# Macaron block on one core: joint quantised norms of two tiles, biases added by GpSimd, scales as two-tensor operations of VectorE

## The chip, the cores and the metric

The kernel runs on one core of a Trainium2 chip. The metric is the device time of one execution in microseconds (us). A time is given as the median of several runs, and one further execution was taken with the hardware profiler. "TensorE" is PE in the profile (its weight loads are PEld), "VectorE" is DVE, "ScalarE" is ACT, "GpSimd" is POOL, and SP is the engine that issues nearly all DMAs.

## The reference, cut to what matters

The input x is 4 x 4096 x 512 in float32, which is 128 tiles of 128 rows. Three sublayers follow each other, each on a layer norm of x:

```python
x = x + 0.5 * ffn(layernorm(x), weight, bias)
x = x + attention(layernorm(x), qkv_w, qkv_b, rpb, proj_w, proj_b)
x = x + 0.5 * ffn(layernorm(x), weight, bias)      # the same weights again

def ffn(x, weight, bias):
    xq, xs = mx_quantize(x)          # blocks of 32 columns: scale = max|block| / 7.5,
    wq, ws = mx_quantize(weight)     # values rounded to the nearest of the FP6 (E2M3) grid
    return (xq * xs) @ (wq * ws).T + bias
```

The attention has 16 heads of 32 columns. Each query sees the 13 keys around it, with a relative bias `rpb`, a softmax, and an output projection by `proj_w` with bias `proj_b`.

## The kernel before, in words

**Products.** Every large product is done in float16 with each operand split into a high and a low part. `product` (L147) issues 12 matmuls of 128x512 into one PSUM tile: low by high, high by low, high by high, four chunks of 128 columns each. Where it has a bias, a thirteenth matmul goes first (L151): a matrix of ones times a bfloat16 tile whose first three rows hold the bias split in three. The FFN (result tile pmf) and the output projection (pmo) have this, the values (pmv) and queries and keys (pmqk) do not. All these results share three PSUM tiles.

**Order of the work.** The order on every engine is written out by hand. The program is a list of slots; a stage is a generator that begins in a slot and says, with each `yield n, rank`, how many slots later it goes on and at which rank within that slot. `run_slot` (L170) runs what is due, lowest rank first, and the engines execute in that order. One step is `STEP = 7` slots, and one tile begins in each step. In the even stretch each step holds stages of several tiles: the first FFN of one tile, the values of an earlier one, an attention item (a group of 512 rows and 4 heads: scores ps at L408, a softmax, the product with the values pv at L478), the output projection of a tile some 13 steps older, and that tile's second FFN.

**The quantised norm.** Both FFNs use `quantised_norm` (L216), once for each tile and FFN. The first FFN's norm is called n1, the second's n3; the plain norm in front of the attention is n2. The stages of one quantised norm are these:

- VectorE: moments of x (L185, L187).
- GpSimd: three operations on one column, giving scale and shift (`factors`, L193, L196, L198).
- ScalarE: the normed tile y (L203).
- VectorE: the greatest magnitude of each block of 32 (L226), a `tensor_scalar` that makes the block's scale of it (L227), a reciprocal (L231).
- GpSimd: y times the reciprocal (L233).
- ScalarE: rounding by a cast to fp8 (L236).
- GpSimd: the fp8 values times the scale (L238).
- ScalarE: the high part (`high`, L208).
- VectorE: the low part (`low`, L213), after which SP issues a DMA that transposes both parts (L214). TensorE reads the transposed tile, xT.

n1 begins 11 slots before its tile's own slot and its product comes 8 slots after its transpose. n3 follows the projection: `project_out` (L516) evicts pmo into x (L525, VectorE) and goes on with the norm in the same stage. The second FFN begins `F2 = 12` slots after the projection, which leaves three slots between the transpose of n3 and the first weight load of its product. n1 and n3 of a step are separate chains of instructions, a slot apart or interleaved. Where this text says "the low part" it means L213, of n1, n2 or n3.

**The softmax.** For each item VectorE adds up the scores from PSUM with the table (L433, L436), takes the maximum of each block (L440), GpSimd subtracts it (L442), ScalarE takes the exponential (L444), VectorE sums (L447), takes the reciprocal (L448) and scales it by a constant with a `tensor_scalar` (L449), GpSimd multiplies (L451), ScalarE writes the high part twice (L455, L456) and GpSimd the low part (L458). SP then transposes the probabilities (pT, L460). The values come back from DRAM by the loads called vs (L384).

**Setup.** Before the slots begin, the FFN weights are quantised (L674 to L720), and `put_bias` (L579) splits the FFN bias in three bfloat16 rows (L583, L585) and sends each into `ffn_bias` by a DMA (L586); the same is done for the attention's bias at L767 to L770.

Of the kernel before, what the change touches and what calls it, by code (L numbers as in the profile page):

```python
# [37 lines left out]
P = 128  # L38
# [12 lines left out]
QB = 32  # L51
# [13 lines left out]
def macaron_kernel(  # L65
# [41 lines left out]

    nudge = const.tile([P, 1], F32, name="nudge")
    nc.gpsimd.memset(nudge, -(2.0 ** -28) * (1 + 2.0 ** -10))
    minus_half = const.tile([P, 1], F32, name="minus_half")  # L110
    nc.gpsimd.memset(minus_half, -0.5)


    wt = const.tile([P, 2, KC, 5 * dim], F16, name="wt")


    ones = const.tile([P, P], BF16, name="ones")
    nc.gpsimd.memset(ones, 1.0)
    ffn_bias = const.tile([P, dim], BF16, name="ffn_bias")
    att_bias = const.tile([P, dim], BF16, name="att_bias")  # L120
    nc.gpsimd.memset(ffn_bias, 0.0)
    nc.gpsimd.memset(att_bias, 0.0)
    qk_b = const.tile([P, 2, KC], F32, name="qk_b")
    coef = const.tile([P, 4], F32, name="coef")
    cf, cp, alpha = coef[:, 0:1], coef[:, 1:2], coef[:, 2:3]
# [4 lines left out]
    def bc(t, n):  # L130

        return t.unsqueeze(2).to_broadcast([t.shape[0], t.shape[1], n])

    def blocks(t):
        return t.rearrange("p (n q) -> p n q", q=QB)
# [8 lines left out]
        ti = t.bitcast(I32)  # L144
        nc.vector.tensor_scalar(ti, ti, 1, None, ALU.bitwise_or)

    def product(pm, lhs, rhs, bias=None):  # L147

        n = 0
        if bias is not None:  # L150
            nc.tensor.matmul(pm, ones, bias, start=True, stop=False)  # L151
            n = 1
        last = n + 3 * KC - 1
        for a, b in ((0, 1), (1, 0), (0, 0)):
            for c in range(KC):
                nc.tensor.matmul(  # L156
                    pm, lhs(a, c), rhs(b, c), start=(n == 0), stop=(n == last)
                )
                n += 1

# [6 lines left out]
    def begin(slot, stage, rank=5):  # L167
        slots.setdefault(slot, []).append((rank, stage))
# [11 lines left out]
        xs[t] = xp.tile([P, dim], F32, tag="x", name=f"x{t}")  # L180
        nc.sync.dma_start(out=xs[t], in_=xf[t * P : (t + 1) * P, :])

    def statistics(t, which):
        st = sm.tile([P, 6], F32, tag=f"st{which}", name=f"st{which}_{t}")
        nc.vector.bn_stats(st, xs[t])  # L185
        mv = sm.tile([P, 2], F32, tag=f"mv{which}", name=f"mv{which}_{t}")
        nc.vector.bn_aggr(mv, st)  # L187
        return mv

    def factors(t, which, mv):  # L190

        rs = sm.tile([P, 1], F32, tag=f"rs{which}", name=f"rs{which}_{t}")
        nc.gpsimd.tensor_scalar(  # L193
            rs, mv[:, 1:2], XS ** -2, LN_EPS * XS ** -2, ALU.mult, ALU.add
        )
        nc.gpsimd.tensor_tensor(rs, rs, minus_half, ALU.pow)  # L196
        nb = sm.tile([P, 1], F32, tag=f"nb{which}", name=f"nb{which}_{t}")
        nc.gpsimd.tensor_scalar(nb, mv[:, 0:1], rs, -1.0, ALU.mult, ALU.mult)  # L198
        return rs, nb

    def normed(t, which, rs, nb):
        y = yp.tile([P, dim], F32, tag=f"y{which}", bufs=1 if which == "n2" else 2, name=f"y{which}_{t}")
        nc.scalar.activation(y, xs[t], AF.Identity, bias=nb, scale=rs)  # L203
        return y

    def high(y, which, t):
        hl = hlp.tile([P, 2, dim], F16, tag=f"hl{which}", name=f"hl{which}_{t}")
        nc.scalar.copy(hl[:, 0, :], y)  # L208
        return hl

    def low(y, hl, dst):

        nc.vector.tensor_tensor(hl[:, 1, :], y, hl[:, 0, :], ALU.subtract)  # L213
        nc.sync.dma_start_transpose(out=dst, in_=hl.rearrange("p s k -> p (s k)"))  # L214

    def quantised_norm(t, which, wait=1):  # L216

        mv = statistics(t, which)
        yield wait, 1
        rs, nb = factors(t, which, mv)  # L220
        yield 1, 1
        y = normed(t, which, rs, nb)
        yield 1, 1
        yb = blocks(y)
        sc = sm.tile([P, NB], F32, tag=f"sc{which}", name=f"sc{which}_{t}")
        nc.vector.tensor_reduce(sc, yb, AX.X, ALU.max, apply_absolute_value=True)  # L226
        nc.vector.tensor_scalar(  # L227
            sc, sc, F8_SCALE / Q_MAX, F8_SCALE * XS * Q_EPS, ALU.mult, ALU.max
        )
        r = sm.tile([P, NB], F32, tag=f"r{which}", name=f"r{which}_{t}")  # L230
        nc.vector.reciprocal(r, sc)  # L231
        yield 1, 1
        nc.gpsimd.tensor_tensor(yb, yb, bc(r, QB), ALU.mult)  # L233
        yield 1, 1
        q8 = q8p.tile([P, dim], F8, tag=f"q8{which}", name=f"q8_{which}_{t}")
        nc.scalar.activation(q8, y, AF.Identity, bias=nudge, saturate=False)  # L236
        yield 1, 3
        nc.gpsimd.tensor_tensor(yb, blocks(q8), bc(sc, QB), ALU.mult)  # L238
        yield 1, 3
        hl = high(y, which, t)  # L240
        yield 1, 1
        xT = xtp.tile([P, 2, KC, P], F16, tag=f"xT{which}", name=f"xT{which}_{t}")
        low(y, hl, xT.rearrange("p s c q -> p (s c) q"))
        ys[t] = xT

    def ffn(t, which):

        xT = ys.pop(t)
        pm = ps_m.tile([P, dim], F32, tag="mm", name=f"pm{which}_{t}")
        product(  # L250
            pm, lambda s, c: xT[:, s, c, :], lambda s, c: wt[:, s, c, FO : FO + dim], ffn_bias
        )
        yield 1, 8
        nc.vector.scalar_tensor_tensor(xs[t], pm, cf, xs[t], ALU.mult, ALU.add)  # L254

    def first_half(t):

        yield from ffn(t, "f1")
        mv = statistics(t, "n2")
        yield 2, 2  # L260
        rs, nb = factors(t, "n2", mv)
        yield 1, 2
        y = normed(t, "n2", rs, nb)
        hl = high(y, "n2", t)
        yield 1, 2
        g, i = divmod(t, GROUP)
        if i == 0:
            x2[g] = x2p.tile([P, 2, KC, GROUP, P], F16, tag="x2", name=f"x2_{g}")
        low(y, hl, x2[g][:, :, :, i, :].rearrange("p s c q -> p (s c) q"))
# [122 lines left out]
    def softmax(m):  # L392
# [53 lines left out]
        total = sm.tile([P, MAXB], F32, tag="total", name=f"total{m}")  # L446
        nc.vector.tensor_reduce(total[:, :n], s, AX.X, ALU.add)  # L447
        nc.vector.reciprocal(total[:, :n], total[:, :n])  # L448
        nc.vector.tensor_scalar(total[:, :n], total[:, :n], PS, None, ALU.mult)  # L449
        yield 1, 4  # L450
        nc.gpsimd.tensor_tensor(s, s, bc(total[:, :n], KN), ALU.mult)  # L451
        yield 2, 8
# [60 lines left out]
                ALU.mult, ALU.subtract,  # L513
            )

    def project_out(t):  # L516

        r = t * P % RING
        pm = ps_m.tile([P, dim], F32, tag="mm", name=f"pmo_{t}")
        product(  # L520
            pm, lambda s, c: ring[:, s, c, r : r + P], lambda s, c: wt[:, s, c, PO : PO + dim],
            att_bias,
        )
        yield 1, 8
        nc.vector.scalar_tensor_tensor(xs[t], pm, cp, xs[t], ALU.mult, ALU.add)  # L525
        yield from quantised_norm(t, "n3")

    def second_half(t):

# [5 lines left out]

    F1, V, QK, SC, PV, OUT, F2 = 6, 2 * STEP + 1, 5 * STEP + 3, 6 * STEP, 8 * STEP + 3, 13 * STEP + 2, 12

    def one(f, *args):
        f(*args)
        return  # L540
        yield

    free = (n_items - 1) * STEP + PV + 3
    for t in range(NT):
        k = t * STEP
        begin(k - 18, one(load, t), 0)
        begin(k - 11, quantised_norm(t, "n1", 2), 1)
        begin(k + F1, first_half(t))
        begin(k + V, values(t))

        at = k + OUT
        if at > free:
            at = free + 4 * ((at - free) // STEP)
        begin(at, project_out(t))
        begin(at + F2, second_half(t))
    for m in range(n_items):
        k = m * STEP
        begin(k + QK, project_qk(m))
        begin(k + SC, softmax(m), 6)
        begin(k + PV, attend(m), 6)  # L560
# [7 lines left out]
    with tc.tile_pool(name="setup", bufs=1) as sp, tc.tile_pool(name="scratch", bufs=2) as scr:  # L568
# [2 lines left out]
        rp = sp.tile([HEADS, NREL + 2 * (QR - 1)], F32, name="rp")  # L571
        for o in range(KC):
            nc.sync.dma_start(out=fw[:, o, :], in_=ffn_w[o * P : (o + 1) * P, :])
        fb = sp.tile([1, dim], F32, name="fb")
        pb_ = sp.tile([1, dim], F32, name="pb_")
        nc.scalar.dma_start(out=fb, in_=ffn_b.unsqueeze(0))
        nc.scalar.dma_start(out=pb_, in_=proj_b.unsqueeze(0))

        def put_bias(out, b, name):  # L579

            for i in range(3):
                part = sp.tile([1, dim], BF16, name=f"{name}{i}")
                nc.vector.tensor_copy(part, b)  # L583
                if i < 2:
                    nc.vector.tensor_tensor(b, b, part, ALU.subtract)  # L585
                nc.sync.dma_start(out=out[i : i + 1, :], in_=part)  # L586

        nc.scalar.dma_start(out=b12, in_=qkv_b.rearrange("(c p) -> c p", p=P))
        nc.gpsimd.memset(rp, 0.0)
        nc.scalar.dma_start(out=rp[:, QR - 1 : QR - 1 + NREL], in_=rpb)  # L590
# [56 lines left out]

        powers(4, 5)
        nc.vector.tensor_scalar(cf, down[:, 4:5], 0.5 / XS, None, ALU.mult)
        nc.vector.tensor_scalar(fb, fb, up[:1, 4:5], XS, ALU.mult, ALU.mult)  # L650
        put_bias(ffn_bias, fb, "fb")

        def put_weights(o, hl):
            return nc.sync.dma_start_transpose(
# [103 lines left out]
        def attention_bias():  # L758
# [5 lines left out]
            pmb = ps_m.tile([P, dim], F32, tag="mm", name="pmb")  # L764
            product(pmb, lambda s, c: vbx[:, s, c, :], lambda s, c: wt[:, s, c, PO : PO + dim])
            yield 1, 9
            for e in (su[:1, 2:3], su[:1, 3:4], XS):  # L767
                nc.vector.tensor_scalar(pb_, pb_, e, None, ALU.mult)
            nc.vector.tensor_tensor(pb_, pmb[:1, :], pb_, ALU.add)
            put_bias(att_bias, pb_, "ab")  # L770

# [93 lines left out]
```

## Time and profile before

| what | value |
|---|---|
| median of three runs | 2516.75 us (2513.81 to 2518.8) |
| the profiled execution | 2513.41 us, of which 2511.3 us is the span from first to last instruction |
| granted TensorE clock, mean of the span | 0.986 |
| TensorE, busy | 2382.7 us (95%) |
| VectorE, busy | 2148.2 us (86%) |
| GpSimd, busy | 1601.0 us (64%) |
| ScalarE, busy | 1370.1 us (55%) |
| DMA queue q1, share of 16 engines | 78.0% |

The shares are averages over the whole span. The first 250 us or so (setup, and the first tiles, whose attention has not begun) and the last 170 us (no new tiles) run differently from the long even stretch between them, in which one step of seven slots follows the other. Numbers of a group (line, engine, operation, tiles) give the count, the total busy time and the mean duration of one instruction; the latter includes any time in which the instruction had begun and stood still.

### The profile page before, as it was taken

The numbers are of one execution on the slowest core, as the hardware profiler recorded it, in microseconds if no ns is written. First come the engines' busy times: TensorE is split into PE (matmuls) and PEld (weight loads), VectorE is DVE, ScalarE is ACT, GpSimd is POOL, SyncE is SP. The second block draws the span as 40 slices with busy tenths as digits, with TensorE's granted clock in tenths as the row PEclk, the third lists the DMA queues.
The fourth block names the chain that finished last, engine by engine and source line by source line (L and its number), as shares of the span: only waits on it lengthen the run. The fifth ranks groups of instructions, "written<-read, shape, count | busy, mean of one in ns | idle before, by whom it ended". The sixth has DMA issues, their size and how long they took to land.

```text
span 2511.3 us, 84309 instructions
## 1 busy us (share of the span) xinstructions
PE 2382.7 (95%) x35923; PEld 1158.1 (46%) x35923; DVE 2148.2 (86%) x4052; ACT 1370.1 (55%) x2306; POOL 1601.0 (64%) x2082
## 2 busy tenths in 40 slices
PE   1799999999999999999999999999999999999877
PEld 0244444444444444444444444444444444444432
DVE  8688998989988898898988889888998989888654
ACT  4455555555555555555555555555555555555432
POOL 4456666666666666666666666666666666666443
PEclk9899999999999999999999999999999999999988
DMA  6589888788878878887887887787888789877752
GB/s 162 123 138 142 151 152 153 144 148 153 152 138 151 152 143 148 155 146 141 154 155 138 147 156 144 149 152 149 143 149 155 142 149 154 153 141 139 120 85 70
DMA packets 929237, 360.22 MB, mean 143 GB/s; under 512 B 722654, under 2 KB 893530, under 8 KB 928860
## 3 DMA queue, kind: packets, MB, share of 16 engines
q1 hardware_dynamic: 928800, 354.81, 78.0%
q8 instruction: 281, 4.60, 0.8%
q14 instruction: 96, 0.79, 0.1%
q10 hardware_dynamic: 60, 0.01, 0.0%
HBM read 109.62 MB, written 67.29 MB: 70 GB/s over the span
## 4 chain that ended last, share of the span: by engine, by line
PE 80%; DVE 10%; DMA 6%; ACT 2%; issue 1%; POOL 1%; SPq 0%; ACTq 0%; DVEq 0%; POOLq 0%
PE pmf L156 22%; PE pmqk L156 22%; PE pmv L156 13%; PE pmo L156 12%; PE ps L408 6%; DMA xTn<-hln 5%; PE pv L478 3%; PE pmf L151 2%; DMA x<-hln 2%; DVE stn L185 1%; DVE scn L227 1%; PE pmo L151 1%; DVE scn L226 1%; DVE x L254 1%; ACT qk L344 1%
## 5 line engine op out<-in xcount | busy, mean ns | idle before, releaser
L156 PE MATMUL pmf<-wt,xTn 128*128 128x512 f16 x3072 | 723.0, 386 | 56.9 <-DMA xTn<-hln 56.8
L156 PE MATMUL pmqk<-x,wt 128*128 128x512 f16 x3072 | 705.9, 380 | 0.0
L156 PEld LDWEIGHTS <-xTn 128*128 128x128 f16 x3072 | 302.7, 99 | 437.7 <-DMA xTn<-hln 70.0
L156 PEld LDWEIGHTS <-wt 128*128 128x128 f16 x3072 | 290.6, 98 | 337.1 <-issue 1.5
L156 PE MATMUL pmv<-wt,x 128*128 128x512 f16 x1536 | 365.0, 389 | 23.6 <-DMA x<-hln 23.0
L458 POOL TENSOR_TENSOR p<-sf,p 128x714 f16<-128x714 f32 (+2 forms) x128 | 192.1, 1501 | 265.5 <-ACT p L455 265.5
L233 POOL TENSOR_TENSOR yn<-yn,rn 128x512 f32<-128x512 f32 x256 | 270.0, 1055 | 132.3 <-DVE rn L231 127.8
L156 PE MATMUL pmo<-wt,ring 128*128 128x512 f16 x1536 | 352.7, 379 | 0.6 <-issue 0.4
L236 ACT ACTIVATE q_n<-yn,nudge 128x512 fp8e4<-128x512 f32 x256 | 184.8, 722 | 292.5 <-POOL yn L233 292.5
L505 ACT ACTIVATE ring<-pv 128x510 f16<-128x510 f32 (+8 forms) x224 | 82.4, 414 | 470.5 <-PE pv L478 468.9
L203 ACT ACTIVATE yn<-x,nbn,rsn 128x512 f32<-128x512 f32 x384 | 313.8, 817 | 37.5 <-POOL nbn L198 37.5
L193 POOL TENSOR_SCALAR rsn<-mvn 128x1 f32<-128x1 f32 x384 | 122.5, 319 | 309.7 <-DVE mvn L187 299.1
L196 POOL TENSOR_TENSOR rsn<-rsn,minus_half 128x1 f32<-128x1 f32 x384 | 252.4, 657 | 32.0
L185 DVE BATCH_NORM_STATS2 stn<-x 128x6 f32<-128x512 f32 x384 | 265.2, 691 | 8.8
L348 DVE SCALAR_TENSOR_TENSOR qk<-pmqk,qk_b,qk 128x512 f16<-128x512 f32 x256 | 191.2, 747 | 89.9 <-ACT qk L344 89.9
L238 POOL TENSOR_TENSOR yn<-q_n,scn 128x512 f32<-128x512 fp8e4 x256 | 263.1, 1046 | 3.3 <-ACT q_n L236 3.3
L213 DVE TENSOR_TENSOR hln<-yn,hln 128x512 f16<-128x512 f32 x384 | 250.5, 678 | 5.4 <-ACT hln L208 4.9
L227 DVE TENSOR_SCALAR scn<-scn 128x16 f32<-128x16 f32 x256 | 241.3, 943 | 8.8
L451 POOL TENSOR_TENSOR sf<-sf,total 128x714 f32<-128x714 f32 (+2 forms) x128 | 178.6, 1395 | 96.8 <-DVE total L449 90.0
L156 PEld LDWEIGHTS <-ring 128*128 128x128 f16 x1536 | 150.1, 98 | 182.7 <-issue 2.4
L208 ACT CAST hln<-yn 128x512 f16<-128x512 f32 x384 | 225.3, 616 | 9.5 <-POOL yn L238 3.2
L156 PEld LDWEIGHTS <-x 128*128 128x128 f16 x1536 | 142.5, 99 | 189.2 <-DMA x<-hln 25.7
(114 smaller groups left out, 3042.0 us busy)
## 6 DMA issues: line engine op xcount, KB each, us to landing
vs<-vd SPq DMA_DIRECT2D x144, 357.0 KB
x<-in_L_attn_x_dram SPq DMA_DIRECT2D x128, 256.0 KB
vd<-vt SPq DMA_DIRECT2D x128, 256.0 KB
out_dram<-x SPq DMA_DIRECT2D x128, 256.0 KB
vs<-vd SPq DMA_DIRECT2D x24, 378.0 KB
vs<-vd SPq DMA_DIRECT2D x24, 315.0 KB
xTn<-hln SPq DMA_TRANSPOSE x256
rows<-in_L_attn_qkv_w_dram SPq DMA_DIRECT2D x12, 256.0 KB
```

What stands on the lines that cost most here:

```text
L156: nc.tensor.matmul(pm, lhs(a, c), rhs(b, c), start=(n == 0), stop=(n == last))
L185: nc.vector.bn_stats(st, xs[t])
L196: nc.gpsimd.tensor_tensor(rs, rs, minus_half, ALU.pow)
L203: nc.scalar.activation(y, xs[t], AF.Identity, bias=nb, scale=rs)
L208: nc.scalar.copy(hl[:, 0, :], y)
L213: nc.vector.tensor_tensor(hl[:, 1, :], y, hl[:, 0, :], ALU.subtract)
L227: nc.vector.tensor_scalar(sc, sc, F8_SCALE / Q_MAX, F8_SCALE * XS * Q_EPS, ALU.mult, ALU.max)
L233: nc.gpsimd.tensor_tensor(yb, yb, bc(r, QB), ALU.mult)
L236: nc.scalar.activation(q8, y, AF.Identity, bias=nudge, saturate=False)
L238: nc.gpsimd.tensor_tensor(yb, blocks(q8), bc(sc, QB), ALU.mult)
L348: nc.vector.scalar_tensor_tensor(t[:, s, 1, KN:], pms[s], bias, t[:, s, 0, KN:], ALU.add, ALU.subtract)
L458: nc.gpsimd.tensor_tensor(p[:, :n, KN : 2 * KN], s, ph, ALU.subtract)
```

## The change

Three things are changed together.

- **Joint norms.** n1 of one tile and n3 of another, where both fall into the same slot, become one piece of work (`quantised_norms`). The moments of each tile are still taken separately (`moments`), into one tile of two columns. From there on each stage handles both: the factors on two columns (four GpSimd operations instead of two times three), two ScalarE activations into one y of 128x1024, and then single operations on 1024 columns or 32 block scales, and one DMA that transposes 16 blocks. At the start of the program, where there is no n3 yet, and at its end, where there is no n1, a joint tile holds one tile.
- **Biases.** The bias matmuls go, and the setup that split the biases. The half FFN bias and the attention's bias are kept in float32 in all partitions, and GpSimd adds them to x (`add_bias`): three operations of 128x512 a tile, one ahead of each addition of a sublayer's result.
- **Scales.** The two `tensor_scalar` operations of VectorE (L227 and L449) become a `scalar_tensor_tensor` with the constant tile `least` and a `tensor_tensor` with the constant tile `p_scale`.

```diff
@@ product
-    def product(pm, lhs, rhs, bias=None):
+    def product(pm, lhs, rhs):
         n = 0
-        if bias is not None:
-            nc.tensor.matmul(pm, ones, bias, start=True, stop=False)
-            n = 1
@@ factors
-    def factors(t, which, mv):
+    def factors(t, which, mv, n=1):
         nc.gpsimd.tensor_scalar(
-            rs, mv[:, 1:2], XS ** -2, LN_EPS * XS ** -2, ALU.mult, ALU.add
+            rs, mv[:, :n, 1], XS ** -2, LN_EPS * XS ** -2, ALU.mult, ALU.add
         )
-        nc.gpsimd.tensor_tensor(rs, rs, minus_half, ALU.pow)
+        nc.gpsimd.tensor_tensor(rs, rs, minus_half[:, :n], ALU.pow)
+        if n == 1:
+            nc.gpsimd.tensor_scalar(nb, mv[:, 0, 0:1], rs, -1.0, ALU.mult, ALU.mult)
+        else:
+            nc.gpsimd.tensor_tensor(nb, mv[:, :n, 0], rs, ALU.mult)
+            nc.gpsimd.tensor_scalar(nb, nb, -1.0, None, ALU.mult)
@@ the quantised norm
-    def quantised_norm(t, which, wait=1):
-        mv = statistics(t, which)
-        yield wait, 1
-        rs, nb = factors(t, which, mv)
+    def quantised_norms(slot):
+        tiles, mv = together.pop(slot)
+        n = len(tiles)
+        rs, nb = factors(slot, "q", mv[0], n)
         yield 1, 1
-        y = normed(t, which, rs, nb)
+        y = yp.tile([P, 2, dim], F32, tag="yq", bufs=2, name=f"yq{slot}")[:, :n]
+        for u, (t, _) in enumerate(tiles):
+            nc.scalar.activation(
+                y[:, u], xs[t], AF.Identity, bias=nb[:, u : u + 1], scale=rs[:, u : u + 1]
+            )
         yield 1, 1
         nc.vector.tensor_reduce(sc, yb, AX.X, ALU.max, apply_absolute_value=True)
-        nc.vector.tensor_scalar(
-            sc, sc, F8_SCALE / Q_MAX, F8_SCALE * XS * Q_EPS, ALU.mult, ALU.max
+        nc.vector.scalar_tensor_tensor(
+            sc, sc, F8_SCALE / Q_MAX, least[:, : n * NB], ALU.mult, ALU.max
         )
...
+        high(y, hl)
         yield 1, 1
-        low(y, hl, xT.rearrange("p s c q -> p (s c) q"))
-        ys[t] = xT
+        low(y, hl, xT[:, :n].rearrange("p u s c q -> p (u s c) q"))
+        for u, (t, _) in enumerate(tiles):
+            ys[t] = xT[:, u]
@@ softmax
-        nc.vector.tensor_scalar(total[:, :n], total[:, :n], PS, None, ALU.mult)
+        nc.vector.tensor_tensor(total[:, :n], total[:, :n], p_scale[:, :n], ALU.mult)
@@ project_out
-        yield from quantised_norm(t, "n3")
+        moments(slot, t, "n3")
@@ the slots
+    def add_bias(t, b):
+        nc.gpsimd.tensor_tensor(xs[t], xs[t], b, ALU.add)
...
-        begin(k - 11, quantised_norm(t, "n1", 2), 1)
+        enlist(k - 10, t, "n1")
+        begin(k - 11, one(moments, k - 10, t, "n1"), 1)
         begin(k + F1, first_half(t))
         begin(k + V, values(t))
+        begin(k + F1 - 1, one(add_bias, t, half_ffn_b), 8)
...
-        begin(at, project_out(t))
+        begin(at - 5, one(add_bias, t, after_b), 8)
+        enlist(at + 2, t, "n3")
+        begin(at, project_out(t, at + 2))
+        begin(at + F2 - 6, one(add_bias, t, half_ffn_b), 8)
         begin(at + F2, second_half(t))
+    for slot in together:
+        begin(slot, quantised_norms(slot), 1)
@@ setup
-        nc.scalar.dma_start(out=fb, in_=ffn_b.unsqueeze(0))
-        nc.scalar.dma_start(out=pb_, in_=proj_b.unsqueeze(0))
+        nc.scalar.dma_start(out=half_ffn_b, in_=ffn_b.partition_broadcast(P))
+        nc.scalar.dma_start(out=after_b, in_=proj_b.partition_broadcast(P))
...
-        put_bias(ffn_bias, fb, "fb")
+        nc.gpsimd.tensor_scalar(half_ffn_b, half_ffn_b, 0.5, None, ALU.mult)
...
-            for e in (su[:1, 2:3], su[:1, 3:4], XS):
-                nc.vector.tensor_scalar(pb_, pb_, e, None, ALU.mult)
-            nc.vector.tensor_tensor(pb_, pmb[:1, :], pb_, ALU.add)
-            put_bias(att_bias, pb_, "ab")
+            nc.vector.scalar_tensor_tensor(after_b, pmb, cp, after_b, ALU.mult, ALU.add)
```

On VectorE the joint low part stays directly behind the moments of n3, as the low part of n3 did. On SP the transpose of the joint tile stands where that of n3 stood, ahead of n2's, and n1's own transpose behind n2's is gone. On GpSimd a step's order becomes: joint factors, two additions, softmax low part, joint multiply by the reciprocal, subtraction of the maximum, the third addition, n2's factors, joint multiply by the scale, multiply by the softmax scale.

## The prediction

> **What bounds the kernel now.** I read the page first, then the table by stretches, the chain of waits, the waits of the even stretch (300 to 2330 us) and the timeline of single steps.
>
> ```profile
> PE 2382.7 (95%) x35923; PEld 1158.1 (46%) x35923; DVE 2148.2 (86%) x4052; ACT 1370.1 (55%) x2306; POOL 1601.0 (64%) x2082
> ...
> PE   1799999999999999999999999999999999999877
> ...
> DMA  6589888788878878887887887787888789877752
> ```
>
> TensorE is full in all but the ends. The table by stretches says the same: 398.13 of 400 us in 1000 to 1400, granted clock 1.00, with DVE 356.72 (16.3 us a step), POOL 266.92 (12.2) and the DMA engines at 0.83. A step of seven slots repeats every 18.24 us in the chain, which there is TensorE alone:
>
> ```profile
> 1014.07 0.21 PE pmo L151
> 1014.28 2.59 PE pmo L156 x12
> ...
> 1022.78 0.21 PE pmf L151
> 1023.00 2.59 PE pmf L156 x12
> 1025.59 0.22 PE pmf L151
> 1025.81 2.59 PE pmf L156 x12
> ```
>
> Here a bias matmul (L151) takes 0.216 us of the array, not the 381 ns of its group's row, which counts overlapping ends. So 384 of them are 83 us, and three a step are 0.65 us.
>
> ```profile
> DVE x L525 <- PE pmo L156: 4.7, 8, 1.5
> ...
> PE pmf L156 <- DMA xTn<-hln: 4.4, 9, 0.9
> ```
>
> These waits of the even stretch are what matters. In two directions nothing is to spare: VectorE reaches the eviction of pmo (L525) as late as TensorE ends it, and TensorE has begun to wait for the transposed n3 tile.
>
> ```profile
> 1018.75 1.27 DVE L213 TENSOR_TENSOR hln<-yn,hln 128x512 f16<-128x512 f32 x2
> ...
> 1019.46 1.29 SPq L214 DMA_TRANSPOSE xTn<-hln  x1
> ...
> 1024.27 1.49 POOL L458 TENSOR_TENSOR p<-sf,p 128x714 f16<-128x714 f32 x1 [1.92 <-ACT p L455]
> ...
> 1024.92 0.88 DVE L227 TENSOR_SCALAR scn<-scn 128x16 f32<-128x16 f32 x1
> ...
> 1033.91 0.18 DVE L449 TENSOR_SCALAR total<-total 128x17 f32<-128x17 f32 x1
> ```
>
> The n3 transpose is issued at 1019.46; its product pmf starts at 1025.64. The trace holds the landing of each issue: over the 109 n3 transposes of the even stretch it comes 4.6 us after the issue in the median (3.2 least, 6.6 at the 95th hundredth), and from landing to the first weight load 1.4 us are left in the median, under 0.8 in a quarter of the steps, 0.04 at worst.
>
> **The change, part by part.**
>
> *Bias matmuls removed:* in the even stretch 18.24 - 0.65 = 17.59 us a step if TensorE stays the bound. About 112 steps have both kinds of tile (n3 joins at step 14, n1 ends at step 127), so 73 us at most.
>
> *Work added and saved.* GpSimd gets three additions 128x512 a step. No row shows one; L233 (1055 ns) and L238 (1046) have the same size with a repeated operand, so I take 1.05 us. The lower bound is 0.53 (L121, a memset of that size, which reads nothing), the upper 1.5 (L705's 1458 in the setup, beside VectorE); loop 2 below holds one of them, -0.5 or +0.4. One factor group of four small instructions takes the place of two groups of three, -1.1 us. Sum 12.2 + 3.15 - 1.1 - 0.2 = 14.0 us of 17.6 (12.5 to 15.4 by the bounds). VectorE loses two L227 (943 ns each) and one start each of L226, L231 and L213; it gains one short operation on 32 columns: 16.3 - 1.9 - 0.45 + 0.2 = 14.2 us. By sums everything fits under 17.59. The order does not make it so easy; two loops have to be walked.
>
> *Loop 1, the joint transpose.* SP now sends n3 and n1 of a step as one transpose of 16 blocks, and n3 is wanted three slots later as before. Late by: the low part (L213) for 1024 columns instead of 512, +0.53 us (1.04 ns a column); 16 blocks instead of 8, +1.15 us (pT's 17 blocks issue in 2452 ns against 1260, and land in 4.4 us at the quartile when nothing else is in the way, against 3.2). Wanted earlier by two bias matmuls, 0.43. In hand: VectorE, with less to do, can take pmo as soon as it ends, -0.2. Sum 1.9 us against margins of 1.4 in the median. Taken over the 109 margins, the mean of what is missing is 0.69 us a step. The step becomes 17.59 + 0.69 = 18.28: the matmuls' gain is gone. Bounds: if the second half of a transpose cost only 0.6 us, 0.35 would be missing (17.95); if it queued at double cost, 1.5 (19.1). The n2 transpose is queued behind it on SP, about 1.1 us later; it has 9 us (issued 1002.31, pmv at 1011.30) and lands in 4.2. pT and the vs loads keep their places.
>
> *Loop 2, VectorE and GpSimd by turns.* Durations are starts to starts in the timeline. From the start of L525: moments, then the low part at +1.58. GpSimd's factors cannot run under it: at 1037.17 L193 takes 0.55 instead of 0.19 and ends with the first L213. Their end comes at 4.4 (before 3.6, +0.53 for the longer L213, +0.27 for a fourth operation). Call it F. ScalarE makes both normed tiles (1.58), then L344 (0.58) and L455 (0.78): L458 on GpSimd begins at F+3.1 and ends at F+4.6. VectorE's reduction of 1024 columns ends at F+4.25; the scale after it comes through at F+4.6, the reciprocal at F+5.0. GpSimd: multiply 128x1024 (1.93, by the 1.72 ns a column between L233 and L442), L442 (1.39), ending at F+8.4; then the new addition (1.05), n2's factors (1.14), and from F+10.6 to F+12.5 the second multiply. VectorE meanwhile does L440 to L448, 6.14 us from the reciprocal's start, and reaches the scale of the softmax sums (L449) at F+10.8.
>
> **Here a rule decides.** The setup shows the case:
>
> ```profile
> 11.39 1.42 POOL L705 TENSOR_TENSOR wu<-wqh,w_hi 128x512 f32<-128x512 f16 x1 [1.28 <-DVE wqh L702]
> 11.83 1.07 DVE L672 TENSOR_TENSOR w_lo<-w_sc,w_hi 128x64 f32<-128x64 f32 x1
> ```
>
> L672 is 64 columns (its like, L681, takes 0.22 us) and ends at 12.90, just after GpSimd's 12.81. L227 above is the same picture for the old form: 0.88 us, ending with L458. The Trainium skill's page "SBUF — State Buffer", section "Who interferes with whom", says that a VectorE instruction with two SBUF inputs shuts out, or is shut out by, a GpSimd instruction that reads SBUF, for its whole length. The new scales have two SBUF inputs. So the change of form does not leave the lock; it moves who waits where. L449 stood clear of GpSimd's work before (174 to 179 ns in every form); now it arrives 0.2 us after the second multiply starts. Held, it ends at F+12.55, and vt, n1's statistics and the next L525 follow 1.42 later: 4.4 + 12.55 + 1.42 = 18.4 us a step. Not held (what the new form would be worth without the rule): 4.4 + 10.8 + 1.5 = 16.7, and loop 1 alone rules. A late pmf from loop 1 makes ps late and with it L449, which pushes it further into the multiply; so I take it as held. With both loops near 18.3 and the margins scattering, a step of 18.5 is my value.
>
> *Setup and end.* The splitting of the two biases leaves VectorE: L650, L583, L585 (0.5 + 2.1 + 1.3) in the first 45 us, where it is the chain, and 100.68 to 105.16 in the chain less one 0.7 eviction: -7.7. Against it two broadcast loads of 256 KB ahead of b12 on ScalarE's queue (0 to +3, the 1 MB of weights beside them is awaited at 6.2). At the end the chain loses some ten bias matmuls (-2.5) and gains additions of 1.05 on GpSimd behind the last tiles (0 to +3). Together -8, from -11 to -2.
>
> *Sum.* 112 x (18.50 - 18.26) = +27; -8; +19 on the profiled execution's 2513.4 us, so 2532. The median of the three runs (2516.75) is 3 us above that execution: 2535.
>
> **The rivals.**
> - *Faster.* The joint transpose lands in time, because its second half is mostly hidden in the issue or because VectorE takes pmo at once, and L449 slips in front of the multiply (by 0.2 us). Step 17.95, 112 x -0.31 - 8 = -43: 2474; with no wait at all 17.59, 2436. For it: the sums of the engines, and L449's near miss. Against: the 1.4 us margin, which the change overdraws by its own size. It decides where the extra delay stays below some 1.6 us.
> - *No difference.* L449 is not held, but the transpose is as late as reckoned: 18.28, +2 - 8: 2511.
> - *Slower by much.* The locks compound: the wide low part is itself held by a GpSimd multiply, or the vs loads queue before the joint transpose (6.6 us landings become 8). Step 19.1, +94 - 8: 2603.
> - That the change doesn't do what it says: the instruction order shows all three parts; excluded.
>
> **How the numbers follow.** My forecast 0.42 (2535), slower by much 0.20, no difference 0.12, faster 0.26. Low end 2468: the faster case with one late transpose in two; high end 2608: the slower case. What is left out is the fully hidden case and steps over 19.2. Within 0.2% (5 us, about what measuring this kernel can tell): 0.09. Faster 0.29, slower 0.62.
>
> **What would show it.** Right: TensorE waits for the joint transpose (pmf <- DMA) some 60 to 100 us in the even stretch instead of 4.4; the softmax scale on VectorE has 1 us or more in place of 0.18; L525's successor no longer follows TensorE at once; the step 18.4 to 18.7. The single bias row is gone and TensorE's busy share near 91%. Wrong: a chain of TensorE alone with steps of 17.6; or a short softmax scale; or GpSimd as the chain.

## The result, and the profile after

| kernel | median | ratio to before, 95% interval |
|---|---|---|
| before | 2517.78 us (2513.81 to 2518.97, 4 runs) | |
| changed | 2548.64 us (2545.11 to 2549.8, 4 runs) | 1.0123 [1.0105, 1.0141] |

The change makes the kernel slower by 31 us, or 1.2%. The forecast was 2535 us, with a range of 2468 to 2608 and a chance of 0.62 for slower. The profiled execution took 2545.11 us, its span is 2543.3 us.

The page of the changed kernel first: busy times, then the rows of TensorE and of the DMA engines over 40 slices, then the chain's shares.

```profile
PE 2324.6 (91%) x35539; PEld 1117.6 (44%) x35539; DVE 2103.4 (83%) x3588; ACT 1341.4 (53%) x2080; POOL 1995.1 (78%) x2012
...
PE   1698999999999999999999999999999999999876
...
DMA  6578787787777779777777877787786788777742
...
DVE 43%; PE 18%; issue 10%; DMA 10%; POOL 10%; ACT 8%; SPq 0%; POOLq 0%; DVEq 0%; ACTq 0%
```

TensorE lost 58 us of work (384 bias matmuls are gone) and yet the span grew: it is no longer full. GpSimd gained 394 us. The chain is VectorE's, with GpSimd, the DMAs and time of issue behind it. The waits of the even stretch (300 to 2330 us; columns: total us, times, longest):

```profile
PEld L151 <- DMA xT<-hlq: 115.0, 92, 3.4
PE pmf L151 <- DMA xT<-hlq: 64.5, 62, 2.9
...
DVE x L539 <- PE pmo L151: 1.9, 5, 0.5
```

TensorE waits for the transposed tile 64.5 us instead of 4.4, and VectorE almost never waits for pmo (1.9 us; 4.7 before): it comes later than TensorE. The timeline of one step shows what VectorE does instead. (L464 is the softmax scale, L449 before; L246 is the joint multiply by the scale; L539 evicts pmo, L525 before.)

```profile
1019.48 0.89 DVE L462 TENSOR_REDUCE total<-sf 128x17 f32<-128x714 f32 x1
...
1020.40 0.27 DVE L463 RECIPROCAL total<-total 128x17 f32<-128x17 f32 x1
1020.44 1.91 POOL L246 TENSOR_TENSOR yq<-q,sc 128x1024 f32<-128x1024 fp8e4 x1
1020.70 1.68 DVE L464 TENSOR_TENSOR total<-total,p_scale 128x17 f32<-128x17 f32 x1
...
1022.30 0.68 DVE L301 TENSOR_TENSOR vt<-pmv,vt 128x512 f16<-128x512 f32 x1
...
1022.53 1.39 POOL L466 TENSOR_TENSOR sf<-sf,total 128x714 f32<-128x714 f32 x1 [0.18 <-DVE total L464]
...
1022.90 0.68 DVE L180 BATCH_NORM_STATS2 stn<-x 128x6 f32<-128x512 f32 x1
...
1023.72 0.72 DVE L539 SCALAR_TENSOR_TENSOR x<-pmo,coef,x 128x512 f32<-128x512 f32 x1
```

L464 handles 17 columns. It begins 0.26 us after GpSimd's multiply and ends at 1022.38, 0.03 us after the multiply does (1022.35). Everything behind it on VectorE, vt, n1's statistics (the first L180) and the eviction, is late by that. The reciprocal (L463) overlaps with the same multiply and keeps its 0.27 us. In 71 items of the even stretch the group of L464 says the same (count, then total us and mean ns of one):

```profile
L464 DVE TENSOR_TENSOR total<-total,p_scale 128x17 f32<-128x17 f32 x71 | 124.1, 1747 | 2.4
```

Before, it took 176 ns. The place where the 32 us of the span were lost is found by the times at which VectorE begins to evict pmo, tile by tile, worked out from the two traces:

| pmo of tile | before | changed | difference |
|---|---|---|---|
| 0 | 228.7 | 241.9 | +13.2 |
| 14 | 483.9 | 502.4 | +18.5 |
| 114 | 2320.5 | 2352.5 | +32.0 |
| end | 2511.3 | 2543.3 | +32.0 |

So 18.5 us are lost before the even stretch is reached, 13.5 us in the hundred steps of it (18.50 us a step against 18.37 in the mean), and nothing at the end.

### The profile page after: what moved, and what is told of

Same layout as the page of the kernel before. It is cut to its first block, busy times and chain, and to the rows that moved or that the text cites. A ratio compares the mean times of both kernels' runs of the same rounds, so it can differ in the third digit from the quotient of the medians.

```text
span 2543.3 us, 82353 instructions
## 1 busy us (share of the span) xinstructions
PE 2324.6 (91%) x35539; PEld 1117.6 (44%) x35539; DVE 2103.4 (83%) x3588; ACT 1341.4 (53%) x2080; POOL 1995.1 (78%) x2012
## 3 DMA queue, kind: packets, MB, share of 16 engines
q8 instruction: 278, 4.55, 0.7%
## 4 chain that ended last, share of the span: by engine, by line
DVE 43%; PE 18%; issue 10%; DMA 10%; POOL 10%; ACT 8%; SPq 0%; POOLq 0%; DVEq 0%; ACTq 0%
DVE stn L180 8%; DMA xT<-hlq 7%; PE pmf L151 6%; ACT yq L228 5%; DVE sc L234 4%; PE pmv L151 4%; DVE x L266 4%; DVE sf L448 4%; POOL rsq L186 3%; POOL rsq L189 3%; DVE sf L451 3%; PE pmqk L151 3%; DVE total L462 3%; DVE vt L301 3%; DVE x L539 3%
## 5 line engine op out<-in xcount | busy, mean ns | idle before, releaser
L151 PE MATMUL pmf<-wt,xT 128*128 128x512 f16 x3048 | 716.5, 388 | 117.7 <-DMA xT<-hlq 109.0
L151 PEld LDWEIGHTS <-xT 128*128 128x128 f16 x3048 | 294.9, 99 | 515.7 <-DMA xT<-hlq 166.3
L244 ACT ACTIVATE q<-yq,nudge 128x1024 fp8e4<-128x1024 f32 (+1 forms) x141 | 150.0, 1064 | 424.2 <-POOL yq L241 424.2
L553 POOL TENSOR_TENSOR x<-x,half_ffn_b 128x512 f32<-128x512 f32 x256 | 326.6, 1276 | 0.0
L186 POOL TENSOR_SCALAR rsq<-mv 128x2 f32<-128x2 f32 (+1 forms) x141 | 133.6, 948 | 242.7 <-DVE mv L181 241.9
L241 POOL TENSOR_TENSOR yq<-yq,r 128x1024 f32<-128x1024 f32 (+1 forms) x141 | 247.3, 1754 | 77.1 <-DVE r L239 75.2
L228 ACT ACTIVATE yq<-x,nbq,rsq 128x512 f32<-128x512 f32 x254 | 194.6, 808 | 159.5 <-POOL nbq L195 121.4
L180 DVE BATCH_NORM_STATS2 stn<-x 128x6 f32<-128x512 f32 x384 | 264.8, 689 | 8.8
L246 POOL TENSOR_TENSOR yq<-q,sc 128x1024 f32<-128x1024 fp8e4 (+1 forms) x141 | 245.0, 1737 | 0.0
L266 DVE SCALAR_TENSOR_TENSOR x<-pmf,coef,x 128x512 f32<-128x512 f32 x256 | 186.5, 729 | 39.2 <-PE pmf L151 39.1
L464 DVE TENSOR_TENSOR total<-total,p_scale 128x17 f32<-128x17 f32 (+2 forms) x128 | 187.7, 1466 | 4.4
L423 PEld LDWEIGHTS <-qk 32*32 32x32 f16 x17536 | 156.0, 89 | 61.8 <-issue 55.0
```

The costliest lines, as they stand in the source:

```text
L151: nc.tensor.matmul(pm, lhs(a, c), rhs(b, c), start=(n == 0), stop=(n == 3 * KC - 1))
L186: nc.gpsimd.tensor_scalar(rs, mv[:, :n, 1], XS ** -2, LN_EPS * XS ** -2, ALU.mult, ALU.add)
L228: nc.scalar.activation(y[:, u], xs[t], AF.Identity, bias=nb[:, u : u + 1], scale=rs[:, u : u + 1])
L246: nc.gpsimd.tensor_tensor(yb, q8.rearrange("p u (n q) -> p (u n) q", q=QB), bc(sc, QB), ALU.mult)
L464: nc.vector.tensor_tensor(total[:, :n], total[:, :n], p_scale[:, :n], ALU.mult)
L553: nc.gpsimd.tensor_tensor(xs[t], xs[t], b, ALU.add)
```

## The experiments

The theory: the softmax scale, held by the joint multiply, sets the even stretch, and the transpose is only the second limit. The main rival: the joint transpose sets it and the held scale has slack. For the ramp, which the forecast had as a gain, theories were formed on the way. Each experiment is an edit of the changed kernel, except the one with the biases alone. The table holds the times, and from each trace (one profiled execution) the start of pmo's eviction of tile 0 (the ramp) and the step between tiles 14 and 114 (mean, and median in brackets).

| kernel | median us | ratio, 95% interval | tile 0 | step |
|---|---|---|---|---|
| before | 2517.78 | | 228.7 | 18.37 (18.32) |
| changed | 2548.64 | 1.0123 [1.0105, 1.0141] | 241.9 | 18.50 (18.46) |
| e1 no softmax scale | 2498.47 | 0.9930 [0.9904, 0.9956] | 242.9 | 18.09 (17.80) |
| e2 split transpose | 2545.59 | 1.0102 [1.0086, 1.0117] | 242.2 | 18.51 (18.42) |
| e3 both | 2483.32 | 0.9859 [0.9845, 0.9874] | 239.9 | 17.97 (17.74) |
| e4 biases alone | 2529.62 | 1.0049 [1.0032, 1.0066] | 224.4 | 18.47 (18.05) |
| e5 joint norms and forms alone | 2535.96 | 1.0073 [1.0058, 1.0088] | 244.9 | 18.40 (18.27) |
| e6 one-tensor scales | 2546.86 | 1.0121 [1.0104, 1.0139] | 243.4 | 18.53 (18.45) |
| e7 early statistics | 2491.98 | 0.9897 [0.9880, 0.9915] | 238.4 | 18.05 (17.82) |
| e8 e3 with early statistics | 2483.37 | 0.9863 [0.9848, 0.9878] | 235.2 | 18.00 (17.73) |
| e9 ramp slots | 2528.30 | 1.0047 [1.0029, 1.0066] | 224.5 | 18.52 (18.45) |
| e10 e8 with ramp slots | 2467.97 | 0.9804 [0.9787, 0.9821] | 226.3 | 17.97 (17.73) |
| e11 e7 with ramp slots | 2479.77 | 0.9856 [0.9832, 0.9880] | 220.8 | 18.06 (17.81) |
| e12 e11 with split transpose | 2465.55 | 0.9793 [0.9777, 0.9810] | 221.0 | 17.95 (17.79) |

**e1, no softmax scale.**

```diff
-        nc.vector.tensor_tensor(total[:, :n], total[:, :n], p_scale[:, :n], ALU.mult)
...
-                ring[:, 0, c, r : r + k], pv[:, u, at : at + k], AF.Copy, scale=1.0 / PS
+                ring[:, 0, c, r : r + k], pv[:, u, at : at + k], AF.Copy, scale=1.0
```

> The changed kernel without the scale of the softmax sums (L464) and with 1.0 in place of 1.0 / PS in the two ring operations; the output differs only in how p is rounded. Theory A (VectorE and GpSimd by turns): in the changed kernel this 17-column operation takes 1.78 us beside the 1024-column multiply of GpSimd and sets the 18.45 us step. Without it VectorE goes from the reciprocal straight on, the step falls by 0.3 to 0.7 us to what the joint transpose leaves (17.9 to 18.2), the time to 2475 to 2515 us; the TensorE wait of pmf for the transpose stays above 40 us. Theory B (the joint transpose sets the step, the held scale has slack): step stays 18.4 to 18.5, time 2535 to 2550, and the wait of pmf for the transpose does not fall.

An operation of 17 columns is taken out and the kernel is 50 us faster than the changed one, and faster than before. The median step falls by 0.66 us. Theory A gave 2475 to 2515. But its last clause failed: TensorE's wait for the transpose fell as well, with the transposes as they were.

```profile
PEld L151 <- DMA xT<-hlq: 61.4, 67, 3.3
...
PE pmf L151 <- DMA xT<-hlq: 26.4, 31, 2.8
```

So more than half of the 64.5 us were no property of the transpose: VectorE, held, gave the tile to SP late.

**e2, two transposes of the old size.**

```diff
-        low(y, hl, xT[:, :n].rearrange("p u s c q -> p (u s c) q"))
         for u, (t, _) in enumerate(tiles):
             ys[t] = xT[:, u]
+        for u in range(n):
+            if u:
+                yield 1, 1
+            low(y[:, u : u + 1], hl[:, u : u + 1], xT[:, u].rearrange("p s c q -> p (s c) q"))
```

> The changed kernel, still with joint norms, but the last piece (low part and transpose) is done as two of the old size: the n3 tile at the old place, the n1 tile one slot later. Theory A: the waits of pmf for the transpose fall from 64 and 115 us to under 15, but the step stays 18.3 to 18.5, since the held softmax scale sets it; time 2525 to 2550. Theory B: the step falls to 17.7 to 18.1, time 2465 to 2505.

The time is as theory A has it, and the step stays: the transpose's width is not what sets the even stretch. The waits did not vanish:

```profile
PEld L151 <- DMA xT<-hlq: 88.0, 49, 4.5
PE pmf L151 <- DMA xT<-hlq: 57.9, 32, 4.0
```

They are fewer and longer, where the expectation had both under 15 us: that part of it failed. It fits e1: a wait for a DMA need not be due to the DMA.

**e3, both edits.** The diff is that of e1 and e2.

> The two edits together: no scale of the softmax sums, and two transposes of the old size. Theory A with the transpose as the second bound: step 17.6 to 17.9, time 2450 to 2485, below either edit alone, and faster than both kernels. If a third thing (the additions and factors on GpSimd, the width of the multiply) is as late as these two, the step stays above 18.1 and the time above 2500.

The time is 2483 us. Undoing the transpose was worth nothing measurable while the scale was held, and 15 us once it was not. The median step of 17.74 is near the 17.59 that the forecast reckoned for a TensorE that never waits; the mean is 17.97, since some steps take 19 us and more, the cause of which no run here isolates.

**e4, the biases alone.** The kernel before, with `add_bias`, its three calls, the broadcast loads and `product` without bias as in the change; norms apart and one-tensor scales.

```diff
-            pm, lambda s, c: xT[:, s, c, :], lambda s, c: wt[:, s, c, FO : FO + dim], ffn_bias
+            pm, lambda s, c: xT[:, s, c, :], lambda s, c: wt[:, s, c, FO : FO + dim]
...
+        begin(k + F1 - 1, one(add_bias, t, half_ffn_b), 8)
...
+        begin(at - 5, one(add_bias, t, after_b), 8)
         begin(at, project_out(t))
+        begin(at + F2 - 6, one(add_bias, t, half_ffn_b), 8)
```

> The kernel before with the biases by GpSimd alone: no bias matmuls, three additions a step and two broadcast loads in the setup; norms apart and one-tensor scales as before. By the forecast's terms: 0.65 us of TensorE a step goes, the n3 transpose keeps its old length and loses 0.43 of 1.4 us margin: step 17.8 to 18.1 against the 18.37 mean of before, setup -8: 2455 to 2485. If the ramp's loss of 13 to 18 us by tile 14 comes from the biases (broadcast loads beside the weights, additions in the first chain), the pmo evictions of tiles 0 to 14 are 10 to 18 us later here too; if it comes from the joint norms, they are 0 to 8 us earlier.

For the ramp it answered: the biases gain 4.3 us at tile 0, so they are not what the ramp lost. For the time the expectation was wrong by 45 us and more. Taking the bias matmuls from TensorE gives nothing by itself; most steps take either some 17.5 or some 19.4 us, and some over 20. The groups show VectorE's small operations stretched beside a GpSimd that has 3.9 us a step more to do:

```profile
L531 POOL TENSOR_TENSOR x<-x,half_ffn_b 128x512 f32<-128x512 f32 x220 | 280.6, 1275 | 0.0
...
L220 DVE TENSOR_SCALAR scn<-scn 128x16 f32<-128x16 f32 x219 | 195.0, 890 | 7.5
...
L442 DVE TENSOR_SCALAR total<-total 128x17 f32<-128x17 f32 x72 | 37.7, 524 | 2.4
```

L220 was as long before the change (1006 ns), the softmax scale was not (176). That this makes the long steps is likely but wasn't shown.

**e5, joint norms and forms alone.** The changed kernel with the bias matmuls, `put_bias` and the setup of before, and without the three additions; the diff is that of e4 the other way round.

> The changed kernel with its biases back in TensorE (bias matmuls, the split biases in the setup, no additions on GpSimd); joint norms and two-tensor scales stay. Theory A: one 1.27 us addition lies between L246's data and its multiply, so without the additions the multiply starts about 1.3 us earlier and the softmax scale meets only its end: L464 falls from 1.78 us to under 0.8. TensorE is then full again or waits for the transpose: step 18.25 to 18.6, time 2515 to 2560. If the joint norms (and not the biases) are what the ramp loses by, pmo of tile 0 is at 236 to 246 us here too (before 228.7, changed 241.9, biases alone 224.4).

Without the additions the multiply begins earlier, and the softmax scale is clear of it in every item:

```profile
L472 DVE TENSOR_TENSOR total<-total,p_scale 128x17 f32<-128x17 f32 x72 | 13.0, 180 | 2.4
```

The step is 18.27 in the median, which is TensorE with its bias matmuls: it is busy for 1821.7 of the 1830 us from 500 to 2330. So the joint norms alone make no hold: the multiply begins 14.0 us after the eviction of pmo in the median, and 15.2 us with the additions. And pmo of tile 0 comes at 244.9 us: the ramp's loss belongs to the joint norms.

**e6, the old form of the scales.**

```diff
-        nc.vector.tensor_tensor(total[:, :n], total[:, :n], p_scale[:, :n], ALU.mult)
+        nc.vector.tensor_scalar(total[:, :n], total[:, :n], PS, None, ALU.mult)
```

> The changed kernel with the two scales of VectorE back in their old form (tensor_scalar with constants). Theory A (what counts is the meeting with the multiply, both forms are held by it): no difference from the changed kernel, 2535 to 2555, L464 1.6 to 1.9 us in the median. Theory C (the two-tensor form itself is what is held): L464 back at 0.18 us, step 17.8 to 18.1, time 2490 to 2510 as without the scale.

```profile
L464 DVE TENSOR_SCALAR total<-total 128x17 f32<-128x17 f32 x71 | 127.2, 1792 | 2.4
```

The old form is held as long (1792 ns against 1747), and the time is the same. Where the operation meets the multiply, its change of form is worth nothing.

**e7, n1's statistics one slot earlier.** Nothing is taken out; one number changes.

```diff
-        begin(k - 11, one(moments, k - 10, t, "n1"), 1)
+        begin(k - 12, one(moments, k - 10, t, "n1"), 1)
```

> The changed kernel with n1's statistics one slot earlier (k - 12 for k - 11), as far ahead of their factors as in the kernel before. Theory A: in the even stretch these 0.87 us of VectorE then lie ahead of the held softmax scale, inside its wait, and no longer behind it: the step falls by 0.3 to 0.8 us, to what the joint transpose leaves (17.7 to 18.2), with L464 near 1.0 us. The ramp: if its loss comes from factors that follow their statistics too closely, pmo of tile 0 is at 228 to 236 us for 241.9. Time 2465 to 2515. If the hold is not what sets the step: 18.4 to 18.5 still, 2530 to 2550.

This is the sharpest test, since all work stays, and it turns 1.2% slower into 1.0% faster. The timeline of a step:

```profile
1030.02 0.69 DVE L180 BATCH_NORM_STATS2 stn<-x 128x6 f32<-128x512 f32 x1
...
1030.84 0.86 DVE L462 TENSOR_REDUCE total<-sf 128x17 f32<-128x714 f32 x1
...
1030.89 1.91 POOL L246 TENSOR_TENSOR yq<-q,sc 128x1024 f32<-128x1024 fp8e4 x1
...
1031.74 0.27 DVE L463 RECIPROCAL total<-total 128x17 f32<-128x17 f32 x1
1032.04 0.80 DVE L464 TENSOR_TENSOR total<-total,p_scale 128x17 f32<-128x17 f32 x1
...
1033.44 0.75 DVE L539 SCALAR_TENSOR_TENSOR x<-pmo,coef,x 128x512 f32<-128x512 f32 x1
```

n1's statistics now lie ahead of the sum (L462), where VectorE would stand still later. The scale is still held to the end of the multiply (1032.80), but only 0.8 us of it remain, and the eviction follows the scale's end 0.6 us later instead of 1.3. The even stretch from tile 14 to 114 gained 45 us of the 57; at tile 0 the ramp gained 3.5 us, less than was expected. That the gain comes from the hold is supported by e8: without the scale the same move leaves the step as it is, though there little is left between it and a full TensorE.

**e8, e3 with the early statistics.** Both diffs together.

> No softmax scale, two transposes of the old size, and n1's statistics one slot earlier. In the even stretch nothing is held any more, so the step stays at 17.7 to 18.0; the ramp gains what the early statistics gain (0 to 12 us). Time 2465 to 2485, the fastest so far or equal to the version without the early statistics (2483).

The even stretch has nothing more to gain from it, as expected; tile 0 comes 4.7 us earlier, and the time is the same as that of e3.

**e9, the ramp's slots.** What remained was the ramp. A joint norm begins in slot k - 10; n1's factors stood in k - 9 before. So its pieces fall into the same slots as those of n2 of the tile before it, and go first.

```diff
-        enlist(k - 10, t, "n1")
-        begin(k - 11, one(moments, k - 10, t, "n1"), 1)
+        alone = (OUT + 12) // STEP
+        slot, early = (k - 9, k - 11) if t < alone else (k - 10, k - 11)
+        enlist(slot, t, "n1")
+        begin(early, one(moments, slot, t, "n1"), 1)
```

> The changed kernel with the norms of the first 15 n1 tiles, which have no partner, back in the slots of the kernel before (factors at k - 9, statistics at k - 11); from tile 15 on nothing differs. Theory R: the ramp loses because the joint norm stands one slot earlier than n1's norm did, so that its pieces (second multiply, high and low part, transpose) go ahead of those of n2 in every slot, and n2 is the ramp's chain. Then pmo of tile 0 comes at 224 to 231 us for 241.9, the step stays 18.45, and the time is 2527 to 2536. Rival: the loss is the statistics' distance to the factors alone; the early statistics took 3.5 us off at tile 0, so pmo of tile 0 would be at 236 to 240 us and the time 2538 to 2543.

Tile 0 comes at 224.5 us, 17.4 us earlier than in the changed kernel, and 20 us of the time are gone, with the step unchanged. The two timelines show the exchange. The changed kernel first: VectorE's low parts, SP's transposes, and TensorE's product pmv, which waits for n2's.

```profile
94.71 0.72 DVE L204 TENSOR_TENSOR hlq<-yq,hlq 128x512 f16<-128x512 f32 x1 [0.37 <-ACT hlq L200]
...
95.35 0.68 DVE L204 TENSOR_TENSOR hln<-yn,hln 128x512 f16<-128x512 f32 x1
95.49 1.23 SPq L205 DMA_TRANSPOSE xT<-hlq  x1
...
96.82 1.29 SPq L205 DMA_TRANSPOSE x<-hln  x1
...
100.01 5.30 PE L151 MATMUL pmv<-wt,x 128*128 128x512 f16 x12 [5.25 <-DMA x<-hln]
```

With the ramp's slots:

```profile
90.06 0.67 DVE L204 TENSOR_TENSOR hln<-yn,hln 128x512 f16<-128x512 f32 x1
...
90.65 0.68 DVE L204 TENSOR_TENSOR hlq<-yq,hlq 128x512 f16<-128x512 f32 x1
90.76 1.23 SPq L205 DMA_TRANSPOSE x<-hln  x1
...
92.10 1.28 SPq L205 DMA_TRANSPOSE xT<-hlq  x1
...
94.45 4.45 PE L151 MATMUL pmv<-wt,x 128*128 128x512 f16 x12 [3.56 <-DMA x<-hln]
```

Here n2 goes first, and the third pmv starts at 94.45 instead of 100.01. In the changed kernel n2's high part was ready at 94.16, and yet VectorE waited 0.37 us for that of n1, whose low part stands ahead in its order.

The edit also puts one slot more between n1's statistics and its factors. That alone is not the cause: e7 does it too, and gained 3.5 us at tile 0. The granted clock is part of the exchange: from 100 to 150 us it was 0.91 in the changed kernel and 1.00 here, and the twelve matmuls shown took 5.30 us there and 4.45 here. How much of the 17.4 us is waiting and how much is TensorE at a lower clock was not separated.

**e10, e11, e12: the parts put together.** e10 is e8 with the ramp's slots; e11 is e7 with them, so that only slots are moved; e12 is e11 with the two transposes of e2.

> No softmax scale, two transposes of the old size, n1's statistics one slot earlier from tile 15 on, and the first 15 tiles in the slots of the kernel before. If the effects add: 2483 less the ramp's 7 to 14 us: 2468 to 2477, the fastest. If the ramp's edit gives nothing: 2480 to 2486.

> The changed kernel with two moves of slots and nothing else: n1's statistics one slot earlier from tile 15 on, and the first 15 tiles in the slots of the kernel before. If the effects add: 2492 less 7 to 14 us: 2477 to 2486, faster than before by 1.2 to 1.6%. If they don't: 2490 or more.

> The version with the two moves of slots (n1's statistics earlier from tile 15 on, the first 15 tiles in their old slots), and the joint transpose done as two of the old size; the softmax scale stays. It weighs the width of the transpose by itself, with nothing else held. By the forecast's term (0.69 us a step for the joint transpose) the step falls from 18.06 to about 17.6 in the mean and the time to 2425 to 2440. If the width is worth what the two versions without the scale show (0.09 to 0.12 us a step): step 17.93 to 17.98, time 2464 to 2475.

The effects nearly add: e11 takes 69 us off the changed kernel, e7 and e9 alone take 57 and 20. So the change as it stands, in other slots, is 1.4% faster than before. e12 against e11 weighs the joint transpose by itself: 0.11 us a step, as the pair e1 and e3 had it (0.12). e12 computes all that the changed kernel does and has the lowest time, 2.1% under before; e10 is within its interval.

## Why the prediction was right, and where it was not

**Loop 2 was right, piece by piece.** Compared with the step that starts with L539 at 1005.26 in the changed kernel's trace (all counted from there): factors end at 4.55 us (forecast F = 4.4); the softmax low part on GpSimd runs from F+2.9 to F+4.4 (F+3.1 to F+4.6); the subtraction ends at F+8.15 (F+8.4); the second multiply runs from F+10.6 to F+12.5 (the same); the softmax scale begins at F+10.9 (F+10.8); the next L539 comes after 18.46 us (18.4). The decision in it was the rule of the Trainium skill's page "SBUF — State Buffer", section "Who interferes with whom": without it the forecast had 16.7 us for this loop. The trace agrees (1747 ns for 17 columns, ending with the multiply), and so does e1. The exact step is in part luck: the loop was reckoned at 18.4, and the tenth on top was for two loops near 18.3, of which the other proved to be no limit. That the change of form does not leave the lock is shown by e6; the same section lists `tensor_scalar` among the operations that can take the shared ports.

**Loop 1 was mis-sized.** The step that failed is "16 blocks instead of 8, +1.15 us". The traces' semaphores give the landings. At the least a joint transpose does land 1.1 us later than n3's own did before (4.2 us after its issue against 3.2). But in the median of the even stretch, beside the other traffic, it is 4.9 us against 4.6. Of the 0.69 us a step that the forecast had missing, e12 and e11 show 0.11. The sign named for it, a wait of TensorE for the transpose of 60 to 100 us, came (64.5), but e1 and e7 cut it to 26.4 and 28.1 with the joint transpose in place. It showed VectorE's lateness and was no sign of this loop.

**The base of the sum was wrong.** The forecast set 18.50 for the changed step and measured it exactly (18.50). It subtracted 18.26, the step of the chain where TensorE is alone. The mean of before over the same hundred tiles is 18.37, since some of its steps take up to 19.1 us. So the even stretch lost 13.5 us and not 27: 112 times 0.11 us is 12 us of the difference. From 18.37 the forecast's own sum would have been 112 x 0.13 - 8 = +7 us, close to the 5 us that it took for no difference.

**The setup had the wrong sign.** The forecast had -8 us for setup and end. It counted what leaves VectorE and what the broadcast loads cost, and that part was right in sign: e4 and e9 reach tile 0 4.3 and 4.2 us earlier than before. What it left out is the slot: the joint norm stands one slot earlier than n1's norm did. It named n2's transpose as queued behind the joint one, and gave it 9 us of slack. In the even stretch it does have time: it was issued at 1011.45 and pmv began at 1017.50, and it lands in 3.2 us in the median. In the first 250 us n2 is on the chain, and its low part and its transpose wait behind n1's. That is 17.4 us (e9), and tile 14 came 18.5 us late instead of early. The end changed nothing, as reckoned (-2.5, and 0 to +3). The range given for setup and end is also wider than its parts: -7.7, -2.5 and twice 0 to +3 make -10 to -4 and not -11 to -2.

So the forecast lies 14 us under the result by two errors of opposite sign, some 13 us too much in the even stretch and some 26 us too little in the ramp. Its verdict rests on loop 2, which the runs confirm: with the ramp mended (e9) the changed kernel is still slower, by 0.5%. That the slowdown came near the forecast's size is luck, since more than half of it arose in the ramp.

**The rivals.** The faster case asked that the scale slip in front of the multiply by 0.2 us. It did not, and it was nearer than that: in 105 of the 109 items of the even stretch the scale is held, begins 0.08 us after the multiply in the median, and ends 0.03 us after it. e11 reaches 2480 us, near that case's price (2474), in another way: VectorE does something useful ahead of the hold, and the ramp is mended. The additions on GpSimd took 1.27 us each and not 1.05. Only the third lies on the path: the first two end 0.41 us before the softmax low part has its input. The 0.2 us that it was too small by were made up for by the other pieces.

## What to carry to other kernels

Where two engines shut each other out, look at what is queued behind the held instruction, and move work that is ready from behind it to ahead of it: here one slot number was worth 2.2%, more than the whole change cost. A stage that is made common to two streams takes one slot for both; in the phase where only one of them runs, the place of the other may be the wrong one, so reckon the ramp with its own order. Subtract a predicted step from the mean step of the trace, not from its cleanest one, and do not take a wait for a DMA as the DMA's fault until you have seen when it was issued.

## What was not expected of the hardware

- A GpSimd addition of two full operands of 128x512 takes 1.27 us; a multiply of that size with a repeated operand 1.05 us (L233 and L238 before).
- One small operation is held and another is not: beside the joint multiply `tensor_scalar` takes 1792 ns on 17 columns and `tensor_tensor` 1747, as forecast, but a reciprocal of the same 17 columns stays at 266 ns in the mean, and at 0.27 us also where it begins 0.85 us into the multiply (e7's timeline).
- In the even stretch a transpose of 16 blocks lands only 0.3 us later than one of 8 in the same place (4.9 and 4.6 us in the median), though the quickest of each are 1.1 us apart.
